# Energies of four heads in one call, with output and norm as a part of their own, in an attention and feed-forward kernel

## The chip, the cores and the metric

The kernel runs on one core of a Trainium2 chip. A core has five engines, each with its own instruction queue: TensorE (PE, matmuls, with weight loads shown apart as PEld), VectorE (DVE), ScalarE (ACT), GpSimd (POOL) and SyncE (SP, which issues DMAs). PE reads SBUF and writes PSUM, which has eight banks of 128 partitions by 2 KB; DVE and ACT empty them. The metric is the device time of one execution in microseconds (us); lower is better.

## What is computed

Eight sequences of 512 rows by 256 channels go through conditioned attention, and then through a gated mixer with a blend of decaying traces and a ternary feed-forward. Cut to what matters:

```python
y = x @ W[id].T + b[id]                       # conditioned projection
q, k, v = silu(y @ Wq), silu(y @ Wk), y @ Wv  # 16 heads of 16
q, k = [t*cos, t*sin], ...                    # 32 values a head
energy = einsum('bhnd,bhmd->bhnm', q, k) * tril
out = einsum('bhnm,bhmd->bhnd', energy, v) @ Wo * sigmoid(y @ G1 @ G2)
x = x + layernorm(out)
ctx = causal_ema(x); gated = x * sigmoid([x, ctx] @ Wg + bg)
traces = causal_ema(gated * mod[d], tau[d])   # 8 traces
gate = sigmoid(sum_d traces[d] * softmax(blend)[d] @ Wtemp + btemp)
c = layernorm((gelu(x @ Wsoma) * gate) @ Wout)
x = x + bitlinear(silu(bitlinear(c, w_gate)) * bitlinear(c, w_up), w_down)
```

There is no softmax over the energies, so attention is done in chunks of 64 rows: within a chunk by masked energies, and across chunks by a running state (the sum of k times v so far).

## The kernel before

For each sequence b there are three parts, written as Python generators that yield where they need something: `attention(b)`, `cond2(b)` (the mixer with the blend) and `ffn(b)`. A `Plan` (lines 42 to 208) simulates the engines while the program is built: `cost` and the table `MATMULS` give each instruction's duration, `add` also the time that a DMA takes. The loop at lines 1124 to 1156 always goes on with the first part, by rank, whose need is met in the plan: `ffn` has rank (1, b), `cond2` (2, b), `attention` (3, b), and the two set-ups of the weights rank (0, ...). Each engine but SP then gets the order of the plan as its fixed order (`keep`). On the chip an engine therefore works through a list and waits, with all behind it, for whatever its next instruction lacks.

Tiles come from pools of so many buffers: `p1` has one for each tag, `p2` two, `p4` four, `p6` six. PSUM is split into `ps`, four single banks (`bank`), and `ps_t`, one tile of four banks (`four_banks`). The blend takes the four-bank tile four times a sequence (`ptr`, line 972: 16 matmuls of the code, then four operations of DVE that add to `tempT`), the feed-forward four times (`pgu`, line 1066), and the set-ups in between.

Attention works on pairs of 128-row tiles, tp = 0 and 1. `project(t)` (494) makes the keys, queries and values of tile t, `turn(t, i)` (524) transposes the keys or the queries into `kT`/`qT`, `states(t, tok)` (533) adds up the running state (`sts`, `total`). `energies(tp, hh)` (570) does two of the four heads of each group: 32 matmuls into two single banks, `pes`, each multiplying 32 rows (one head's values) by 64 columns, cycling over two row groups `e` and two halves `r` of the chunk rows; then DVE multiplies each bank by the causal mask into `et`. `output(tp)` (591) multiplies energies by values, and queries by states, into two banks `po`, which ACT copies to `aT`. Then follow `pw` (aT by Wo), the gate, the norm and the residual sum into `xs`.

The body of attention (642 to 723) is one sequence: project 0, project 1, turned 0, project 2, turned 1, energies(0, 0), project 3, turned 2, energies(0, 1), output(0), the addition of beta to xs on POOL, turned 3, the gate's matmuls `pg`, energies(1, 0), `pgt`, energies(1, 1), then for tp = 0 `pw` and the norm, output(1), and the same for tp = 1. `head[b]` is set after `pg`, and lets the next sequence's attention start; `tail[b]` is set after output(1), and the next sequence's turned(1) waits for it. `cond2(b)` starts when attention(b) is done.

Of the kernel before, what the change touches and what calls it, by code (L numbers as in the profile page):

```python
# [17 lines left out]
P = 128  # L18
# [23 lines left out]
class Plan:  # L42
# [5 lines left out]

    MATMULS = {"ptr": 0.069, "po": 0.028, "pg": 0.125, "pgt": 0.26, "pm": 0.26}
    TABLES = {AF.Gelu: 1, AF.Silu: 2, AF.Exp: 3, AF.Ln: 4, AF.Sin: 5}  # L50
# [41 lines left out]
    def add(self, engine, op, args, kw, made):  # L92
# [4 lines left out]
        if op == "dma_start":  # L97
            cost = 1.2 if "transpose" in kw else 0.05
            late = math.prod(outs[0].shape) * (4 if outs[0].dtype == F32 else 2) / 230e3
        else:  # L100
            cost = self.cost(engine, op, outs[0], ins, kw)
            if engine == "tensor":
                late = 0.2
# [148 lines left out]
def adaln_attn_ffn_kernel(ctx: ExitStack, tc: tile.TileContext, a: dict, out: bass.AP):  # L252
# [22 lines left out]
    ps_t = pool("ps_t", 1, space=bass.MemoryType.PSUM)  # L275
    p1, p2, p3, p4, p6 = (pool(f"p{n}", n) for n in (1, 2, 3, 4, 6))

# [196 lines left out]
    def attention(b, xs, wt, bt):  # L474
# [19 lines left out]
        def project(t):  # L494

            tp, u = divmod(t, 2)
            pkq = bank(f"pkq_{b}_{t}")
            for k in range(KC):
                te.matmul(
                    pkq, yT[:, k, chunk(t)], wkq[:, k].rearrange("p e c -> p (e c)"), start=k == 0, stop=k == KC - 1  # L500
                )
            pv = bank(f"pv_{b}_{t}")[:, :C]
            for k in range(KC):
                te.matmul(pv, yT[:, k, chunk(t)], wv[:, k, :], start=k == 0, stop=k == KC - 1)
            sg = p2.tile([P, 2, H, HD], F32, tag="sg", name=f"sg_{b}_{t}")
# [18 lines left out]
        def turn(t, i):  # L524

            tp, u = divmod(t, 2)
            n, turned = (("k", kTs[tp]), ("q", qTs[tp]))[i]
            pt = bank(f"p{n}T_{b}_{t}")
            for g in range(NG):
                te.transpose(pt[:, chunk(g)], toks[t, i][:, chunk(g)], ident)  # L530
            ac.copy(turned[:, :, chunk(u)], pt.rearrange("p (g n) -> p g n", n=P))

        def states(t, tok):
# [35 lines left out]

        def energies(tp, hh):  # L570

            kT, qT = kTs[tp], qTs[tp]
            pes = [bank(f"pe_{b}_{tp}_{2 * hh + e}").rearrange("p (g u n) -> p g u n", g=NG, u=2) for e in range(2)]
            for g in range(NG):
                for u in range(2):
                    for e, r in ((0, 0), (1, 1), (0, 1), (1, 0)):
                        rows = slice(32 * (2 * hh + e), 32 * (2 * hh + e + 1))
                        at = slice(P * u + 64 * r, P * u + 64 * (r + 1))
                        te.matmul(
                            pes[e][64 * r : 64 * (r + 1), g, u, :], kT[rows, g, at], qT[rows, g, at], start=True, stop=True  # L580
                        )
            for e in range(2):
                et = p4.tile([P, NG, 2, 64], F32, tag="et", name=f"et_{b}_{tp}_{2 * hh + e}")
                ve.tensor_mul(
                    et.rearrange("p g u n -> p (g u) n"),
                    pes[e].rearrange("p g u n -> p (g u) n"),
                    causal.unsqueeze(1).to_broadcast([P, 2 * NG, 64]),
                )
                ets[tp, hh, e] = et

        def output(tp):
# [21 lines left out]
            for half in range(2):  # L613
                for u in range(2):
                    for e in range(2):
                        for turn in range(2):
                            for pair in range(4):
# [7 lines left out]
                                    vz[rows, u, 2 * g + hh, 2 * e : 2 * e + 2, :].rearrange("p e d -> p (e d)"),  # L625
                                    ets[tp, hh, e][rows, g, u, :],
                                    last=half == 1 and u == 1 and e == 1,
# [5 lines left out]
        def turned(t):  # L633
# [6 lines left out]
            turn(t, 1)  # L640

        project(0)
        yield needs(yT, banks=2)
# [42 lines left out]
        gates = []  # L686
# [4 lines left out]
        yield needs(kTs[1], qTs[1], banks=2)  # L691
        energies(1, 1)

        og = p1.tile([P, NT, C], F32, tag="og", name=f"og_{b}")
        for tp in range(NT // 2):
            t = 2 * tp
            if tp == 1:
                yield needs(ets[1, 1, 0], ets[1, 1, 1], sts[7], banks=2)
                output(1)
                tail[b] = True  # L700
            yield needs(aTs[tp])
            pw = bank(f"pw_{b}_{t}").rearrange("p (t c) -> p t c", t=2)
            for u in range(2):
                for k in range(KC):
                    te.matmul(
                        pw[:, u, :], aTs[tp][:, k, chunk(u)], wo[:, k, :], start=k == 0, stop=k == KC - 1
                    )
            mv = p2.tile([P, 2, 2], F32, tag="mv", name=f"mv_{b}_{t}")
            for u in range(2):

                ve.scalar_tensor_tensor(
                    og[:, t + u, :], gates[u][:, tp, :], 1.0, pw[:, u, :], ALU.add, ALU.mult
                )
                layer_stats(og[:, t + u, :], mv[:, u, :])
            rstd = layer_rstd(mv, f"rstd_a{b}_{t}")
            for u in range(2):
                ve.scalar_tensor_tensor(
                    og[:, t + u, :], og[:, t + u, :], mv[:, u, 0:1], gamma_a, ALU.subtract, ALU.mult
                )
                ve.scalar_tensor_tensor(  # L720
                    xs[:, t + u, :], og[:, t + u, :], rstd[:, u : u + 1], xs[:, t + u, :], ALU.mult, ALU.add
                )
        x2s[b] = xs

# [140 lines left out]
    def cond2(b):  # L865
# [14 lines left out]
        for k in range(KC):  # L880
            for s in range(2):
# [225 lines left out]
    wt_free = [0]  # L1107
    head, tail, begun, done = {}, {}, {}, {}
    for b in range(-1, B):
        head[b] = tail[b] = b < 0  # L1110
        for what in ("attention", "cond2", "ffn"):
            begun[b, what] = done[b, what] = b < 0
# [11 lines left out]
    while True:  # L1124
# [92 lines left out]
```

## Time and profile before

| | us |
|---|---|
| median of 3 runs | 760.28 (754.30 to 762.75) |
| profiled execution, device time | 761.35 |
| its span in the profile | 759.6 |
| PE busy | 651.3 |
| DVE busy | 509.6 |
| ACT busy | 254.4 |
| POOL busy | 216.9 |

The profile is of one execution, whose device time stands beside its span; busy times are for the whole span. Nearly all of the kernel's instructions are issued by one helper, so every row carries the same line, 221, and a group is told by its tiles: `pe<-qT,kT` are the matmuls that write the energies from qT and kT. A matmul in float32 shows as two records. Sizes are partitions by elements; for matmuls the first pair is the part of the PE array that is used (rows by columns). The output blocks, for later comparison:

```profile
L221 PE MATMUL po<-et,vz 64*32 64x64 f32 x2048 | 28.1, 238 | 13.8 <-issue 13.1
L221 DVE SCALAR_TENSOR_TENSOR tempT<-ptr,bw_c,tempT 128x512 f32<-128x512 f32 x128 | 95.8, 749 | 43.4 <-PE ptr L221 38.1
L221 PE MATMUL ptr<-dm,gated 32*128 32x128 f32 x1024 | 42.0, 304 | 21.9 <-DVE tempT L221 21.7
```

After the bar stand the busy time and the mean of one in ns, then the engine's idle time just before these instructions and what ended it.

### The profile page before, as it was taken

To read this page: it belongs to the slowest core of one execution; us is meant where nothing else is said; L and a number is where in the kernel's file an instruction comes from. 1 tells how busy PE (TensorE), PEld (TensorE's weight loads), DVE (VectorE), ACT (ScalarE), POOL (GpSimd) and SP (SyncE) were. 2 spreads that over 40 slices of the span, in tenths; PEclk is the share of its full clock that TensorE was granted. 3 is DMA by queue.
4 is the path that set the end of the run, shared out by engine and by line. 5 is a ranking of instruction groups with operands and counts; after the bars stand their busy time and mean duration, and the time that the engine had idled before them with its cause. 6 is when DMAs were issued, how large, how long until landed. Compare 5 with 4: busy or idle time off the path is not lost.

```text
span 759.6 us, 21112 instructions
## 1 busy us (share of the span) xinstructions
PE 651.3 (86%) x9330; PEld 435.4 (57%) x9330; DVE 509.6 (67%) x1015; ACT 254.4 (33%) x452; POOL 216.9 (29%) x239
## 2 busy tenths in 40 slices
PE   7689999999889988999989988999999997884453
PEld 3466666666655666566756655566766664442221
DVE  7974456876666865786666966686687667666445
ACT  3822332453224423343235322342246321410111
POOL 2740551234124231333133241333133422100000
PEclk9789999999999989999999999999999998886757
DMA  8501000121011110121011200120002100110011
GB/s 270 174 8 40 1 3 3 29 56 57 4 22 43 42 38 2 43 62 38 3 30 42 47 27 17 29 63 9 3 16 56 30 3 16 36 41 7 11 38 48
DMA packets 61196, 28.63 MB, mean 38 GB/s; under 512 B 46346, under 2 KB 60594, under 8 KB 61106
## 3 DMA queue, kind: packets, MB, share of 16 engines
q1 hardware_dynamic: 60146, 26.50, 13.1%
q8 instruction: 73, 1.20, 0.6%
q10 hardware_dynamic: 960, 0.79, 0.3%
q14 instruction: 17, 0.14, 0.1%
HBM read 12.60 MB, written 4.19 MB: 22 GB/s over the span
## 4 chain that ended last, share of the span: by engine, by line
PE 69%; DVE 18%; issue 5%; ACT 4%; DMA 3%; POOL 0%; ACTq 0%; DVEq 0%; SPq 0%; POOLq 0%
PE pgu L221 7%; PE pwg L221 6%; PE ptr L221 5%; PE po L221 5%; PE pkq L221 5%; PE py L221 4%; PE pwo L221 4%; DVE tempT L221 4%; PE ptg L221 4%; PE pd L221 4%; PE pso L221 3%; PE pe L221 3%; PE pw L221 3%; DVE h L221 2%; PE pv L221 2%
## 5 line engine op out<-in xcount | busy, mean ns | idle before, releaser
L221 DVE SCALAR_TENSOR_TENSOR tempT<-ptr,bw_c,tempT 128x512 f32<-128x512 f32 x128 | 95.8, 749 | 43.4 <-PE ptr L221 38.1
L221 POOL TENSOR_TENSOR st<-total,own 128x256 f32<-128x256 f32 x56 | 46.5, 839 | 106.2 <-DVE total L221 105.1
L221 POOL TENSOR_TENSOR ktok<-sg,cs 128x512 f32<-128x512 f32 x32 | 42.3, 1322 | 119.7 <-ACT sg L221 119.7
L221 DVE SCALAR_TENSOR_TENSOR h<-pgu,steps,sig 128x1024 f32<-128x1024 f32 x32 | 41.0, 1282 | 46.2 <-ACT sig L221 46.1
L221 PE MATMUL pkq<-wkq,yT 128*128 128x512 f32 x128 | 64.7, 628 | 0.0
L221 PE MATMUL ptr<-dm,gated 32*128 32x128 f32 x1024 | 42.0, 304 | 21.9 <-DVE tempT L221 21.7
L221 ACT ACTIVATE sig<-pgu,steps 128x1024 f32<-128x1024 f32 x32 | 35.6, 1113 | 65.3 <-PE pgu L221 60.0
L221 PE MATMUL pd<-w_downT,hqT 128*128 128x256 bf16 x256 | 37.4, 295 | 20.6 <-DMA hqT<-hq 20.6
L221 PEld LDWEIGHTS <-cqT 128*128 128x128 bf16 x256 | 26.4, 104 | 49.7 <-issue 14.9
L221 PEld LDWEIGHTS ptr<-dm,gated 32*128 32x128 f32 x1024 | 35.5, 204 | 30.0 <-issue 19.5
L221 PE MATMUL pgu<-w_gateT,cqT 128*128 128x512 bf16 x128 | 37.0, 416 | 16.1 <-DMA cqT<-cq 11.1
L221 POOL TENSOR_TENSOR qtok<-sg,cs 128x512 f32<-128x512 f32 x32 | 49.1, 1534 | 0.0
L221 POOL TENSOR_SCALAR rstd_a<-mv 128x2 f32<-128x2 f32 x16 | 6.8, 422 | 136.0 <-DVE mv L221 126.2
L221 DVE TENSOR_TENSOR et<-pe,causal 128x512 f32<-128x512 f32 x64 | 41.8, 684 | 5.5 <-PE pe L221 5.1
L221 PEld LDWEIGHTS <-hqT 128*128 128x128 bf16 x256 | 25.5, 105 | 33.8 <-DMA hqT<-hq 24.4
L221 PE MATMUL pwo<-woutT,soma 128*128 128x256 f32 x128 | 33.7, 394 | 10.7 <-ACT square L221 9.6
L221 PEld LDWEIGHTS pe<-qT,kT 32*64 32x64 f32 x2048 | 34.9, 135 | 13.7 <-issue 8.4
L221 PE MATMUL pe<-qT,kT 32*64 32x64 f32 x2048 | 40.4, 223 | 2.7 <-DVE et L221 1.1
L221 ACT ACT_TABLE_LOAD x28 | 35.9, 1283 | 19.3 <-PE pgu L221 10.5
L221 PE MATMUL po<-et,vz 64*32 64x64 f32 x2048 | 28.1, 238 | 13.8 <-issue 13.1
L221 DVE TENSOR_REDUCE hmax<-h 128x1 f32<-128x1024 f32 x32 | 38.7, 1210 | 0.3
L221 ACT COPY aT<-po 128x256 f32<-128x256 f32 x32 | 10.3, 375 | 80.3 <-PE po L221 80.3
(189 smaller groups left out, 1335.0 us busy)
## 6 DMA issues: line engine op xcount, KB each, us to landing
x<-in_x_dram SPq DMA_DIRECT2D x8, 512.0 KB, 4.5
out_dram<-res SPq DMA_DIRECT2D x32, 128.0 KB, 1.7
wt<-in_weightT_dram SPq DMA_DIRECT2D x8, 256.0 KB, 2.8
w_gateT_raw<-in_w_gateT_dram SPq DMA_DIRECT2D x2, 512.0 KB, 4.4
w_upT_raw<-in_w_upT_dram SPq DMA_DIRECT2D x2, 512.0 KB, 5.9
w_downT_raw<-in_w_downT_dram SPq DMA_DIRECT2D x2, 512.0 KB, 7.2
wgT<-in_wgT_dram SPq DMA_DIRECT2D x1, 512.0 KB, 5.1
hqT<-hq SPq DMA_TRANSPOSE x32, 2.7
```

The lines of the kernel that those rows point to most:

```text
L221: made = issue(*args, **kw)
```

## The change

Four things are changed together.

1. `energies(tp)` does all four heads of a group in one call of 64 matmuls. It writes them into the four-bank tile, one bank for each head j, and cycles over four row groups, with the two halves alternating. The mask is applied to two banks at a time.
2. Energies, output, `pw`, norm and residual become a generator of their own, `heads()`, started after turned(1) with rank (3, b, 1), behind its own attention and ahead of the next one. `ready` tells it how far the turns and the gates are. The remaining attention is projections, turns, states and gates. `outputs[b]` counts the outputs done: the next sequence's attention starts after one (and `head`), and its turned(2) after two. Energies of b wait for the whole of heads(b - 1), as do the gates; `cond2(b)` starts when heads(b) is done.
3. Buffers: `kT`/`qT` are taken when they are first turned into and not at the projection; `et` is two buffers of twice the size; `st` gets seven buffers in place of six, and `h1` one in place of two.
4. The plan's costs: 0.019 us for a matmul of the energies (the general formula gave 0.034), 0.45 us for SP to issue a DMA (0.05), and 330 GB/s for transfers (230).

```diff
-    MATMULS = {"ptr": 0.069, "po": 0.028, "pg": 0.125, "pgt": 0.26, "pm": 0.26}
+    MATMULS = {"ptr": 0.069, "pe": 0.019, "po": 0.028, "pg": 0.125, "pgt": 0.26, "pm": 0.26}
...
-            cost = 1.2 if "transpose" in kw else 0.05
-            late = math.prod(outs[0].shape) * (4 if outs[0].dtype == F32 else 2) / 230e3
+            cost = 1.2 if "transpose" in kw else 0.45
+            late = math.prod(outs[0].shape) * (4 if outs[0].dtype == F32 else 2) / 330e3
...
-                kTs[tp] = p2.tile([P, NG, 2 * P], F32, tag="kT", name=f"kT_{b}_{tp}")
-                qTs[tp] = p2.tile([P, NG, 2 * P], F32, tag="qT", name=f"qT_{b}_{tp}")
...
-            n, turned = (("k", kTs[tp]), ("q", qTs[tp]))[i]
+            n, turned = (("k", kTs), ("q", qTs))[i]
+            if u == 0:
+                turned[tp] = p2.tile([P, NG, 2 * P], F32, tag=f"{n}T", name=f"{n}T_{b}_{tp}")
...
-                    sts[c] = p6.tile([P, NG, 2, 2 * HD], F32, tag="st", name=f"st_{b}_{c}")
+                    sts[c] = p7.tile([P, NG, 2, 2 * HD], F32, tag="st", name=f"st_{b}_{c}")
...
-        def energies(tp, hh):
+        def energies(tp):
             kT, qT = kTs[tp], qTs[tp]
-            pes = [bank(f"pe_{b}_{tp}_{2 * hh + e}").rearrange("p (g u n) -> p g u n", g=NG, u=2) for e in range(2)]
+            pes = four_banks(f"pe_{b}_{tp}").rearrange("p j (g u n) -> p j g u n", g=NG, u=2)
             for g in range(NG):
                 for u in range(2):
-                    for e, r in ((0, 0), (1, 1), (0, 1), (1, 0)):
-                        rows = slice(32 * (2 * hh + e), 32 * (2 * hh + e + 1))
+                    for turn in range(2):
+                        for j in range(4):
+                            r = (j + turn) % 2
+                            rows = slice(32 * j, 32 * (j + 1))
...
-            for e in range(2):
-                et = p4.tile([P, NG, 2, 64], F32, tag="et", name=f"et_{b}_{tp}_{2 * hh + e}")
+            for hh in range(2):
+                et = p2.tile([P, 2, NG, 2, 64], F32, tag="et", name=f"et_{b}_{tp}_{hh}")
...
+        def heads():
+            for tp in range(NT // 2):
+                yield needs(
+                    kTs.get(tp, xs),
+                    qTs.get(tp, xs),
+                    four=True,
+                    when=lambda: ready["energies"] > tp and written(kTs[tp], qTs[tp]) and done[b - 1, "heads"],
+                )
+                energies(tp)
+                yield needs(ets[tp, 0], ets[tp, 1], sts[4 * tp + 3], banks=2)
+                output(tp)
+                outputs[b] = tp + 1
+                if tp == 0:
+                    gp.tensor_add(xs, xs, beta_a.unsqueeze(1).to_broadcast([P, NT, C]))
+                    og = p1.tile([P, NT, C], F32, tag="og", name=f"og_{b}")
+                yield needs(aTs[tp], when=lambda: ready["gates"])
...
+            x2s[b] = xs
...
         project(2)
-        yield needs(when=lambda: tail[b - 1])
         yield from turned(1)
-        yield needs(kTs[0], qTs[0], banks=2)
-        energies(0, 0)
+        ready["energies"] = 1
+        start((3, b, 1), b, "heads", heads(), lambda: True)
         yield needs(yT, banks=2)
         project(3)
+        yield needs(when=lambda: outputs[b - 1] == 2)
         yield from turned(2)
-        yield needs(kTs[0], qTs[0], banks=2)
-        energies(0, 1)
-        yield needs(ets[0, 1, 0], ets[0, 1, 1], sts[3], banks=2, when=lambda: done[b - 1, "attention"])
-        output(0)
-
-        gp.tensor_add(xs, xs, beta_a.unsqueeze(1).to_broadcast([P, NT, C]))
         yield from turned(3)
+        ready["energies"] = 2
...
         head[b] = True
-        yield needs(kTs[1], qTs[1], banks=2)
-        energies(1, 0)
-        yield needs(g1T, banks=2)
+        yield needs(g1T, banks=2, when=lambda: done[b - 1, "heads"])
...
+        ready["gates"] = True
...
-        h1 = p2.tile([P, T // 2], F32, tag="h1", name=f"h1_{b}")
+        h1 = p1.tile([P, T // 2], F32, tag="h1", name=f"h1_{b}")
...
-        if b < B and b in loaded and head[b - 1]:
+        if b < B and b in loaded and head[b - 1] and outputs[b - 1]:
...
-        if b < B and done[b, "attention"] and done[b - 1, "cond2"] and done[0, "setup_cond2"] and done[0, "setup_ffn"]:
+        if b < B and done[b, "heads"] and done[b - 1, "cond2"] and done[0, "setup_cond2"] and done[0, "setup_ffn"]:
```

More of the change, by code (lines that the diff above doesn't have):

```diff
@@ L275, in adaln_attn_ffn_kernel @@
     ps_t = pool("ps_t", 1, space=bass.MemoryType.PSUM)
-    p1, p2, p3, p4, p6 = (pool(f"p{n}", n) for n in (1, 2, 3, 4, 6))
+    p1, p2, p3, p4, p7 = (pool(f"p{n}", n) for n in (1, 2, 3, 4, 7))
     def bank(name, dtype=F32):
@@ L530, in turn @@
                 te.transpose(pt[:, chunk(g)], toks[t, i][:, chunk(g)], ident)
-            ac.copy(turned[:, :, chunk(u)], pt.rearrange("p (g n) -> p g n", n=P))
+            ac.copy(turned[tp][:, :, chunk(u)], pt.rearrange("p (g n) -> p g n", n=P))
         def states(t, tok):
@@ L568, in attention @@
         ets, aTs = {}, {}
-        def energies(tp, hh):
+        def energies(tp):
             kT, qT = kTs[tp], qTs[tp]
-            pes = [bank(f"pe_{b}_{tp}_{2 * hh + e}").rearrange("p (g u n) -> p g u n", g=NG, u=2) for e in range(2)]
+            pes = four_banks(f"pe_{b}_{tp}").rearrange("p j (g u n) -> p j g u n", g=NG, u=2)
             for g in range(NG):
                 for u in range(2):
-                    for e, r in ((0, 0), (1, 1), (0, 1), (1, 0)):
-                        rows = slice(32 * (2 * hh + e), 32 * (2 * hh + e + 1))
[L578 to L581, printed above, removed]
-            for e in range(2):
-                et = p4.tile([P, NG, 2, 64], F32, tag="et", name=f"et_{b}_{tp}_{2 * hh + e}")
+                    for turn in range(2):
+                        for j in range(4):
+                            r = (j + turn) % 2
+                            rows = slice(32 * j, 32 * (j + 1))
+                            at = slice(P * u + 64 * r, P * u + 64 * (r + 1))
+                            te.matmul(
+                                pes[64 * r : 64 * (r + 1), j, g, u, :], kT[rows, g, at], qT[rows, g, at], start=True, stop=True
+                            )
+            for hh in range(2):
+                et = p2.tile([P, 2, NG, 2, 64], F32, tag="et", name=f"et_{b}_{tp}_{hh}")
                 ve.tensor_mul(
-                    et.rearrange("p g u n -> p (g u) n"),
-                    pes[e].rearrange("p g u n -> p (g u) n"),
-                    causal.unsqueeze(1).to_broadcast([P, 2 * NG, 64]),
+                    et.rearrange("p e g u n -> p (e g u) n"),
+                    pes[:, 2 * hh : 2 * hh + 2].rearrange("p e g u n -> p (e g u) n"),
+                    causal.unsqueeze(1).to_broadcast([P, 4 * NG, 64]),
                 )
-                ets[tp, hh, e] = et
+                ets[tp, hh] = et
         def output(tp):
@@ L625, in output @@
                                     vz[rows, u, 2 * g + hh, 2 * e : 2 * e + 2, :].rearrange("p e d -> p (e d)"),
-                                    ets[tp, hh, e][rows, g, u, :],
+                                    ets[tp, hh][rows, e, g, u, :],
                                     last=half == 1 and u == 1 and e == 1,
@@ L640, in turned @@
             turn(t, 1)
+        gates = []
+        ready = {"energies": 0, "gates": False}
+        def heads():
[5 more added lines that the diff above has]
+                    when=lambda: ready["energies"] > tp and written(kTs[tp], qTs[tp]) and done[b - 1, "heads"],
+                )
+                energies(tp)
[6 more added lines that the diff above has]
+                yield needs(aTs[tp], when=lambda: ready["gates"])
+                t = 2 * tp
+                pw = bank(f"pw_{b}_{t}").rearrange("p (t c) -> p t c", t=2)
+                for u in range(2):
+                    for k in range(KC):
+                        te.matmul(
+                            pw[:, u, :], aTs[tp][:, k, chunk(u)], wo[:, k, :], start=k == 0, stop=k == KC - 1
+                        )
+                mv = p2.tile([P, 2, 2], F32, tag="mv", name=f"mv_{b}_{t}")
+                for u in range(2):
+                    ve.scalar_tensor_tensor(
+                        og[:, t + u, :], gates[u][:, tp, :], 1.0, pw[:, u, :], ALU.add, ALU.mult
+                    )
+                    layer_stats(og[:, t + u, :], mv[:, u, :])
+                rstd = layer_rstd(mv, f"rstd_a{b}_{t}")
+                for u in range(2):
+                    ve.scalar_tensor_tensor(
+                        og[:, t + u, :], og[:, t + u, :], mv[:, u, 0:1], gamma_a, ALU.subtract, ALU.mult
+                    )
+                    ve.scalar_tensor_tensor(
+                        xs[:, t + u, :], og[:, t + u, :], rstd[:, u : u + 1], xs[:, t + u, :], ALU.mult, ALU.add
+                    )
+            x2s[b] = xs
         project(0)
@@ L685, in attention @@
                 te.matmul(pgts[u][:, tp, :], g1T[rows, chunk(tp)], g2[rows, :], start=True, stop=True)
-        gates = []
         for r in range(2):
@@ L690, in attention @@
             gates.append(gate)
[L691 to L723, printed above, removed]
+        ready["gates"] = True
     def setup_cond2():
@@ L1107, in adaln_attn_ffn_kernel @@
     wt_free = [0]
-    head, tail, begun, done = {}, {}, {}, {}
+    head, outputs, begun, done = {}, {}, {}, {}
     for b in range(-1, B):
-        head[b] = tail[b] = b < 0
-        for what in ("attention", "cond2", "ffn"):
+        head[b], outputs[b] = b < 0, 2 * (b < 0)
+        for what in ("attention", "heads", "cond2", "ffn"):
             begun[b, what] = done[b, what] = b < 0
```

## The prediction

> **What bounds the kernel now.** I read the page from the top: span, the 40 slices, the chain, then the groups. After that I asked for busy time by stage, for the waits of PE alone, and for the order of time around a few blocks.
>
> ```profile
> span 759.6 us, 21112 instructions
> PE   7689999999889988999989988999999997884453
> DVE  7974456876666865786666966686687667666445
> PEclk9789999999999989999999999999999998886757
> PE 69%; DVE 18%; issue 5%; ACT 4%; DMA 3%; POOL 0%; ACTq 0%; DVEq 0%; SPq 0%; POOLq 0%
> ```
>
> Each digit is one slice of 19 us. PE is full from slice 4 to slice 33, DVE at six to seven tenths. After that PE falls to half: the last batch's blend and feed-forward run there alone, and no attention is left to fill their gaps. The last line, the chain of waits by engine, has PE at 69%. Split at 85 and 640 us (columns: length, then busy us and count of PE, weight load, DVE, ACT, POOL; then granted clock, DMA share, GB/s):
>
> ```profile
> 0.00:85.00 85.00, 68.37 (x979) 44.80 (x980) 62.27 (x134) 36.61 (x65) 39.14 (x48) 0.90 0.36 110
> 85.00:640.00 555.00, 513.92 (x7996) 353.13 (x7994) 381.99 (x760) 197.55 (x358) 172.28 (x182) 0.98 0.11 28
> 640.00:760.00 120.00, 68.99 (x356) 37.50 (x356) 65.32 (x123) 20.21 (x30) 5.44 (x9) 0.72 0.13 31
> ```
>
> In the middle stage PE works 513.9 of 555 us, so a microsecond of PE work taken out there is nearly a microsecond of the kernel. Its 41.1 us of idle time are small, by PE's own waits in that stage (total, times, longest):
>
> ```profile
> PE ptr L221 <- DVE tempT L221: 11.6, 9, 2.1
> PE po L221 <- issue: 11.0, 8, 2.1
> PE pwo L221 <- ACT square L221: 8.3, 14, 0.6
> ...
> PE pe L221 <- DVE et L221: 1.1, 4, 0.3
> ```
>
> The last 120 us hold no attention, so the change can only move them as a whole.
>
> **The energies' matmuls.** The groups that the change touches, and their nearest neighbours (busy us, mean ns of one, then idle before):
>
> ```profile
> L221 PE MATMUL pe<-qT,kT 32*64 32x64 f32 x2048 | 40.4, 223 | 2.7 <-DVE et L221 1.1 <-DVE total L221 1.0 <-ACT qT L221 0.6
> L221 DVE TENSOR_TENSOR et<-pe,causal 128x512 f32<-128x512 f32 x64 | 41.8, 684 | 5.5 <-PE pe L221 5.1
> L221 DVE SCALAR_TENSOR_TENSOR h<-pgu,steps,sig 128x1024 f32<-128x1024 f32 x32 | 41.0, 1282 | 46.2 <-ACT sig L221 46.1
> ```
>
> A float32 matmul of the code is two records, so 32 calls of 64 records take 40.4 us, 1.26 us each. One block and, for comparison, an output block in the order of time:
>
> ```profile
> 200.39 1.16 PE L221 MATMUL pe<-qT,kT 32*64 32x64 f32 x64
> ...
> 215.39 1.43 PE L221 MATMUL po<-et,vz 64*32 64x64 f32 x122
> 218.93 0.31 PE L221 MATMUL po<-et,vz 64*32 64x64 f32 x6 [2.10 <-issue]
> ```
>
> An energies record takes 1.16/64 = 18 ns, an output record 1.43/122 = 11.7 ns, although both stream 64 columns. The start times inside the blocks say why. In energies four records start 7 ns apart, then 39 ns pass: 59 ns for four, because the code cycles over two row groups by two column halves, four places of the array. Output cycles over eight places, and at its best eight start 7 ns apart with the next eight 57 to 58 ns after the first. The change makes energies cycle over four row groups by two halves, also eight places. So 128 records of a call should come as 16 groups at some 59 ns, what 64 records take now: 16 calls at 1.26 us = 20.2 us instead of 40.4. Bounds: saving 0 if the pace per record stays at 18 ns, 40.4 - 2048 x 13.7 ns = 12.3 us if output's mean over the run holds (28.1 us for 2048 records, slow stretches in it), 20.2 if the best pace holds. I take 20.2: the interleaving is that of output's best stretch, and the operands are stored as in today's block. Where does it land? The energies have 33.65 us of their PE time in the middle stage and 6.75 in the first, by the same windows for them alone. Half of 33.65 is 16.8, taken whole; of the 3.4 in the first stage, where PE is busy 68.4 of 85 us, I count half, 1.7. **Sum: -18.5 us.**
>
> The Trainium skill, page "TensorE: Matmul & The Clock Gate", section "Wait — 56ns, not 53.3ns?", speaks against this: starts of matmuls never come closer than about 25 ns, however small they are. Today's 18 ns and 11.7 ns per record are already below that, so the rows decide; read per matmul of the code, 1024 x 25 ns = 25.6 us would save 5 us less than I say and give 747.
>
> **Fetching instructions.** The 2.10 us before the last six output records are put down to "issue": nothing that the profile shows was awaited. This comes in long runs of short instructions: the instruction queue moves 16 KB blocks, and over the run 73 of them make the 1.20 MB beside 18,660 PE records, some 256 records each. A new energies call is 128 matmuls and 128 weight loads, about one block in 1.2 us. Today's half calls show no such wait of the matmuls before pe. Bounds: 0, or the mean output stall, 11.0/8 = 1.4 us, at all 16 calls, 22 us. I take 0.13 us a call, **+2**, near today's row of none, since the number of instructions is unchanged and slow projections lie between.
>
> **The mask on DVE.** 64 operations at 684 ns become 32 over two banks. Nearest row of that shape is h, 1282 ns: 41.0 instead of 41.8 us. DVE is 69% busy in the middle, so it is counted at nothing; its cover is DVE's 173 us of idle time there.
>
> **The four banks as a meeting place.** Energies leave two of the four single banks and take the one group of four that the blend (ptr) and the feed-forward (pgu) also use. A call holds it for 1.26 us of matmuls and two masks of 1.28 us, with gaps 4 us. The order of PE is fixed ahead, so where the plan believes the group free and DVE is late, PE stands with all behind it: projections, turns, pwo. Today's instance:
>
> ```profile
> 275.90 0.68 DVE L221 TENSOR_TENSOR et<-pe,causal 128x512 f32<-128x512 f32 x1
> 276.13 2.09 PE L221 MATMUL ptr<-dm,gated 32*128 32x128 f32 x32 [2.12 <-DVE tempT L221]
> ```
>
> Here a mask on DVE delayed the blend's own reads, and PE stood 2.12 us. In the middle 28 ptr blocks lose 11.6 us, 0.41 each. The 14 new users there at that rate: **+5.8**; bounds 0 and 14 x 2.12 = 30.
>
> The skill's "TensorEngine Tiling (Array Packing)", section "PSUM Bottleneck", warns that tiling speeds up the matmuls and not the emptying of their banks. The rows agree in kind (1.26 us to fill, 2.6 to empty four banks); were emptying to set the pace everywhere, the saving would vanish and the time stay near 760.
>
> **Energies, output and norm as a part beside.** Projections and turns no longer stand in line with energies and output. The new part may start output(0) while project(3) and later turns wait, and the next batch gets as far as its turned(2) before the old batch's second output, where turned(1) was the limit. In the blend stage PE so has more to put before a late ptr. I take two thirds of the 11.6 us, **-8**; bounds -12 (all of it) and 0. The moves inside it issue what they did: the addition of beta on POOL (8 x 2.42 us, POOL is 29% busy), gates, pw, norm; no DMA changes place on SP's queue. Buffers: kT and qT taken at the turn, one more st, one h1 less. h1's next writer comes about 70 us later, so nothing waits; st gains slack. The new costs of transfers alter the planned order alone. They matter at the start, where PE waits 2.0, 0.7 and 2.5 us for weight sums: bounds -5 and +5, taken 0.
>
> **Sum:** -18.5 + 2 + 5.8 - 8 = -18.7 us. The profiled execution took 761.35 us, 1.75 more than its span, and the median shown is 760.28: 740.9 in the span, 742 on the median.
>
> **Rivals.**
>
> (A) As summed: 742, its own range 733 to 752 (waits and refilling vary). Chance 0.58.
>
> (B) More: all of the ptr waits refilled, no new waits, 2 us at the start: -18.5 - 12 - 2 = -32, 728. For it speaks that only 41 us of the middle are idle and the new part is free to fill them. Against: 8.3 us are waits of pwo for ACT and 11.0 for instructions, which nothing here touches. 0.12.
>
> (C) The eight places bring nothing, since loading weights or fetching limits the pace, as in output's slow stretches: 0 + 2 + 5.8 - 8, so 760. For it: output's mean is 13.7 ns, not 7.4. Against: its best stretches. The change then does not do what it says. 0.14.
>
> (D) Slower: the group of four banks becomes the bound. In the middle, 14 calls hold it 4 us each, 56 us. The blend's four uses follow each other at 4.4 us through a stage of some 17 us (100.7 to 118.3 in the first batch), so it is taken there nearly without a gap, and feed-forward's uses follow soon. If PE stands for half of that: +28 + 2 - 18.5 = +11.5, 772. It decides once PE's waits for DVE before ptr, pgu and pe exceed today's 13 us by about 20. Against: the blend has the higher rank and will take the group first, and PE has projections meanwhile. 0.16.
>
> About 1% (752.7 to 767.9) is what a measurement can tell from no change. Faster: A but its edge 0.56, B 0.12, a little of C 0.04: 0.72. Same: A's edge 0.02, most of C 0.10, D's lower part 0.03: 0.15. Slower: 0.13. The range of 726 to 764 leaves out some 0.04 of B and most of D.
>
> **What would show it.** Right: pe near 20 us in 16 blocks of 128 records at 1.2 to 1.3 us; et 32 times near 1.28 us; PE busy near 631; the middle 15 to 20 us shorter, the last 120 us unchanged. Fetching: "issue" before pe. The meeting place: waits of pe for DVE, and of ptr and pgu for et. It would be wrong if pe stays near 40 us (C), or if PE's idle time in the middle grows beyond 60 us (D).

## The result and the profile after

| | us |
|---|---|
| median after, 20 runs | 764.10 (759.91 to 772.90) |
| median before on the same chip, 20 runs | 759.59 (754.30 to 763.98) |
| after by before, 95% interval | 1.0059 (1.0038 to 1.0080) |
| profiled execution after, device time | 760.01 |
| its span | 758.3 |
| PE busy, and idle within the span | 636.4, 121.9 (before 651.3, 108.3) |

The forecast of 742 was wrong, and 764.1 lies just outside its range: the kernel is 4.5 us slower on the median, 0.6%, small but clear of noise. Medians are of all runs, and ratios leave out the few that ran in a slower state (one of after, one of E6, three of E8, one of the before beside E9 to E12). The two profiled executions differ the other way (760.0 after, among the fastest of its 20, and 761.4 before), so they show what became of the saving and not the last 4.5 us. In them 14.9 us of PE work are gone and PE's idle time is 13.6 us longer. Most of this study asks where that idle time comes from.

The page of the kernel after, span, slices and chain:

```profile
span 758.3 us, 21057 instructions
...
PE   7688999999998989999978999998888856965453
...
DVE  7875445698557967577757957668579854677445
...
PE 67%; DVE 18%; issue 5%; ACT 4%; DMA 3%; POOL 1%; SPq 0%; ACTq 0%; POOLq 0%; DVEq 0%
```

Its groups (busy us, mean ns of one, idle before):

```profile
L221 PE MATMUL pe<-qT,kT 32*64 32x64 f32 x2048 | 25.8, 231 | 1.4 <-issue 1.4
...
L221 DVE TENSOR_TENSOR et<-pe,causal 128x1024 f32<-128x1024 f32 x32 | 38.0, 1216 | 6.6 <-PE pe L221 6.1
```

The energies fell by 14.6 us, the mask by 3.8. By stage (columns as before: length, busy us and count of PE, weight load, DVE, ACT, POOL; clock, DMA share, GB/s):

```profile
0.00:85.00 85.00, 64.27 (x970) 42.15 (x971) 60.79 (x128) 31.92 (x60) 36.89 (x48) 0.88 0.35 110
85.00:640.00 555.00, 502.48 (x7992) 341.50 (x7990) 387.26 (x722) 199.85 (x355) 166.00 (x181) 0.97 0.12 28
640.00:760.00 120.00, 69.63 (x371) 37.93 (x370) 68.54 (x133) 22.43 (x39) 6.14 (x11) 0.76 0.13 31
```

The middle stage holds nearly as many PE records as before, 7992 to 7996, so the same work still needed the same 555 us, with 11.4 us less of it busy. PE's own waits there (total, times, longest):

```profile
PE ptr L221 <- DVE tempT L221: 15.5, 8, 4.8
PE po L221 <- issue: 10.8, 8, 1.6
PE pwo L221 <- ACT square L221: 7.1, 12, 0.6
PE ptg L221 <- DVE tempT L221: 6.0, 3, 2.2
PE pgu L221 <- DVE h L221: 3.9, 3, 1.7
...
PE pe L221 <- issue: 1.4, 1, 1.4
```

No pe waits for a DVE mask, as rival D would have it. What grew are waits inside the blend, `ptr` by 3.9 us and `ptg` to 6.0, and those of the feed-forward's `pgu`, 3.9 (no such row before). Most of the time of `ptr` is lost late: the stretch from 580 to 640 us, before and after:

```profile
580.00:640.00 60.00, 54.37 (x1067) 40.72 (x1065) 41.19 (x86) 17.95 (x37) 18.86 (x21) 0.97 0.07 18
```

```profile
580.00:640.00 60.00, 42.30 (x588) 28.02 (x586) 40.48 (x74) 14.14 (x20) 5.50 (x7) 0.86 0.11 27
```

PE does 12 us less in these 60 us, with half the records and a third of POOL's work: attention has run out. The timelines say why. Each blend opens with `px2T<-ident,x`, the transposes of what attention left in x. DVE writes the last x here, in before and in after:

```profile
643.31 0.88 DVE L221 SCALAR_TENSOR_TENSOR x<-og,rstd_a,x 128x256 f32<-128x256 f32 x2 [0.90 <-POOL rstd_a L221]
```

```profile
622.02 0.48 DVE L221 SCALAR_TENSOR_TENSOR x<-og,rstd_a,x 128x256 f32<-128x256 f32 x1 [0.60 <-POOL rstd_a L221]
623.09 0.47 DVE L221 SCALAR_TENSOR_TENSOR x<-og,rstd_a,x 128x256 f32<-128x256 f32 x1
```

And the last blend on PE begins here, before and after (in the second, the blend ahead of it is shown as well):

```profile
645.05 1.91 PE L221 MATMUL px2T<-ident,x 128*128 128x128 f32 x8
```

```profile
619.91 1.21 PE L221 MATMUL ptr<-dm,gated 32*128 32x128 f32 x32 [2.26 <-DVE tempT L221]
...
625.94 2.09 PE L221 MATMUL ptr<-dm,gated 32*128 32x128 f32 x32 [4.82 <-DVE tempT L221]
631.35 2.09 PE L221 MATMUL ptr<-dm,gated 32*128 32x128 f32 x32 [3.32 <-DVE tempT L221]
...
646.00 1.04 PE L221 MATMUL px2T<-ident,x 128*128 128x128 f32 x8
```

The last attention ends at 623.6 instead of 644.2 us, 20.6 earlier, a little more than the forecast took off the whole kernel. But the last blend does not begin earlier, and its start sets the time: in all 16 traces of this study the span ends 111 to 117 us after it. `cond2(7)` may start only when `cond2(6)` is done, and that one ran late: it began at 578.4, before at 568.1. Its `ptr` stand 2 to 5 us each for DVE, with no attention left to fill them.

Blend 6 is late because its x was (575.4; before 564.5). PE's timeline shows sequence 6 between its first and its second call of energies:

```profile
477.44 1.59 PE L221 MATMUL pe<-qT,kT 32*64 32x64 f32 x128
...
505.41 1.48 PE L221 MATMUL po<-et,vz 64*32 64x64 f32 x128
...
512.64 1.03 PE L221 MATMUL pgu<-w_gateT,cqT 128*128 128x512 bf16 x4
...
523.18 1.17 PE L221 MATMUL ptr<-dm,gated 32*128 32x128 f32 x32
...
531.24 1.29 PE L221 MATMUL ptr<-dm,gated 32*128 32x128 f32 x32 [2.29 <-DVE tempT L221]
...
543.31 1.17 PE L221 MATMUL ptr<-dm,gated 32*128 32x128 f32 x32
...
550.49 1.59 PE L221 MATMUL pe<-qT,kT 32*64 32x64 f32 x128
```

Before, sequence 6 had its four calls within 27 us (517.7 to 545.2). Now 73 us lie between two. The first 33 or so are the new part's own order: `output` and `pw` come between the calls, `pw` at 508.3. In the other 40 its keys and queries are ready (the last copy to `qT` ends at 487.4), and the four-bank tile goes through a series of feed-forward and blend uses. Sequences 1, 2 and 4 have 32, 41 and 73 us there, sequences 3, 5 and 7 34 to 36.

The blends start at 82, 162, 252, 320, 416, 484, 578 and 646 us in after. These intervals of 68 to 96 us are no more uneven than those of before (71 to 99), but what the blends wait for has changed. Before, each begins within 4 us of its last x, and the last `pwo` of the blend ahead (the matmuls that close a blend on PE) has ended 12 to 35 us earlier. In after, blends 2, 4 and 6 begin 3 us after their last x, and 3, 5 and 7 only 21 to 22 us after it, directly behind the `pwo` of the blend ahead.

### The profile page after: what moved, and what is told of

Its sections match the earlier page's. It is cut to its first block, busy times and chain, and to the rows that moved or that the text cites. A ratio compares the mean times of both kernels' runs of the same rounds, so it can differ in the third digit from the quotient of the medians.

```text
span 758.3 us, 21057 instructions
## 1 busy us (share of the span) xinstructions
PE 636.4 (84%) x9330; PEld 421.6 (56%) x9330; DVE 516.6 (68%) x983; ACT 254.2 (34%) x452; POOL 209.0 (28%) x239
## 3 DMA queue, kind: packets, MB, share of 16 engines
q1 hardware_dynamic: 60146, 26.50, 13.7%
## 4 chain that ended last, share of the span: by engine, by line
PE 67%; DVE 18%; issue 5%; ACT 4%; DMA 3%; POOL 1%; SPq 0%; ACTq 0%; POOLq 0%; DVEq 0%
PE pgu L221 8%; PE pwg L221 6%; PE pkq L221 5%; DVE tempT L221 5%; PE ptr L221 4%; PE pwo L221 4%; PE pw L221 4%; PE po L221 4%; PE pso L221 4%; PE ptg L221 4%; PE pd L221 3%; PE py L221 3%; PE pv L221 2%; DVE h L221 2%; PE pe L221 2%
## 5 line engine op out<-in xcount | busy, mean ns | idle before, releaser
L221 PE MATMUL pkq<-wkq,yT 128*128 128x512 f32 x128 | 66.7, 646 | 0.4 <-ACT kT L221 0.4
L221 DVE SCALAR_TENSOR_TENSOR h<-pgu,steps,sig 128x1024 f32<-128x1024 f32 x32 | 41.0, 1282 | 32.9 <-ACT sig L221 32.9
L221 PE MATMUL ptr<-dm,gated 32*128 32x128 f32 x1024 | 41.4, 302 | 22.0 <-DVE tempT L221 19.4
L221 POOL TENSOR_TENSOR st<-total,own 128x256 f32<-128x256 f32 x56 | 43.1, 774 | 58.4 <-DVE total L221 58.3
L221 PE MATMUL pd<-w_downT,hqT 128*128 128x256 bf16 x256 | 39.8, 307 | 22.2 <-DMA hqT<-hq 20.6
L221 PEld LDWEIGHTS ptr<-dm,gated 32*128 32x128 f32 x1024 | 35.0, 203 | 33.9 <-issue 26.2
L221 PEld LDWEIGHTS <-cqT 128*128 128x128 bf16 x256 | 25.8, 103 | 48.0 <-issue 18.6
L221 POOL TENSOR_TENSOR qtok<-sg,cs 128x512 f32<-128x512 f32 x32 | 43.2, 1350 | 0.0
L221 DVE TENSOR_TENSOR et<-pe,causal 128x1024 f32<-128x1024 f32 x32 | 38.0, 1216 | 6.6 <-PE pe L221 6.1
L221 PE MATMUL ptg<-tempT,wtempT 128*128 128x512 f32 x64 | 32.9, 649 | 7.7 <-DVE tempT L221 7.7
L221 DVE TENSOR_REDUCE hmax<-h 128x1 f32<-128x1024 f32 x32 | 38.8, 1214 | 0.4
L221 POOL TENSOR_SCALAR rstd<-squares 128x2 f32<-128x2 f32 x16 | 3.1, 192 | 129.0 <-ACT square L221 129.0
L221 ACT ACTIVATE sg<-pkq 128x512 f32<-128x512 f32 x32 | 19.1, 598 | 57.6 <-PE pkq L221 57.6
L221 PE MATMUL po<-et,vz 64*32 64x64 f32 x2048 | 26.3, 225 | 13.0 <-issue 13.0
L221 ACT COPY qT<-pqT 128x512 f32<-128x512 f32 x32 | 18.7, 586 | 52.7 <-PE pqT L221 52.7
```

The source lines that it names most:

```text
L221: made = issue(*args, **kw)
```

## The experiments

All times are medians against before on the same chip (759.6 to 761.1), ratios with their 95% intervals.

**Which part costs?** Energies of before (two heads a call, two single banks) inside the changed structure; the four-head energies inside the old sequence; the new transfer costs alone in the kernel before; and, in the changed kernel, energies first at the four-bank tile.

E2, from after:

```diff
-    MATMULS = {"ptr": 0.069, "pe": 0.019, "po": 0.028, ...}
+    MATMULS = {"ptr": 0.069, "po": 0.028, ...}
-                    four=True,
+                    banks=2,
-                energies(tp)
-                yield needs(ets[tp, 0], ets[tp, 1], sts[4 * tp + 3], banks=2)
+                energies(tp, 0)
+                yield needs(banks=2)
+                energies(tp, 1)
+                yield needs(ets[tp, 1, 0], ets[tp, 1, 1], sts[4 * tp + 3], banks=2)
```

> The changed kernel with the energies of before: two heads a call in two single banks, two calls for a tile pair, all else as changed. PE's energies return from 25.8 to about 40 us. Theory 1: the group no longer holds the energies up, so in spite of 14 us more of PE work it is no slower than the changed kernel, 745 to 760. Theory 2: the loss stays and the PE work is added: 768 to 780. Theory 3 (the plan's transfers made a worse order): also 768 to 780.

E3, from before (energies as in the change):

```diff
-        yield needs(kTs[0], qTs[0], banks=2)
-        energies(0, 0)
...
-        energies(0, 1)
+        yield needs(kTs[0], qTs[0], four=True)
+        energies(0)
...
-        energies(1, 0)
...
-        energies(1, 1)
+        yield needs(kTs[1], qTs[1], four=True)
+        energies(1)
```

> The kernel before with only the four-head energies in the four-bank group; the body of attention stays one sequence, and transfers are planned as before. Theory 1: the whole attention, projections too, stands behind the group, so it is slower than before, 765 to 790. Theory 2: PE's saving of about 15 us arrives, 742 to 752. Theory 3: as theory 2.

E4, from before:

```diff
-            cost = 1.2 if "transpose" in kw else 0.05
-            late = ... / 230e3
+            cost = 1.2 if "transpose" in kw else 0.45
+            late = ... / 330e3
```

> The kernel before with only the plan's two costs of transfers changed (0.45 us for an issue, 330 GB/s). Theory 3: this alone is slower than before by 8 us or more, 768 to 780. Theories 1 and 2: the order at the start changes a little and the time is within 6 us of before, 754 to 766.

E1, from after:

```diff
+                wants[b] = lambda tp=tp: ready["energies"] > tp and written(kTs[tp], qTs[tp]) and done[b - 1, "heads"]
...
+                del wants[b]
                 energies(tp)
...
-                yield needs(dm, gated, four=True)
+                yield needs(dm, gated, four=True, when=lambda: not wanted())
...
-            yield needs(cqT[:, t], four=True)
+            yield needs(cqT[:, t], four=True, when=lambda: not wanted())
```

> The changed kernel, but blend and feed-forward leave the four-bank group alone whenever a sequence's energies are ready for it. Theory 1 (the energies stand behind the group: in the changed kernel the second energies call of sequence 6 came 73 us after the first, and its x2 at 575 us where the old one had it at 565): the second calls come within 40 us of the first, x2 of sequences 2, 4 and 6 comes 10 us or more earlier, PE's idle time at 580 to 640 us falls from 17.7 us to under 10, and the time falls to 740 to 752. Theory 2 (the part's own order and rank are the loss, not the group): the calls come earlier but the time stays at 757 to 770.

| | us | ratio |
|---|---|---|
| E2 | 779.53 | 1.0287 (1.0207 to 1.0367) |
| E3 | 802.24 | 1.0554 (1.0474 to 1.0634) |
| E4 | 754.08 | 0.9918 (0.9882 to 0.9955) |
| E1 | 773.80 | 1.0174 (1.0092 to 1.0255) |

Four heads at once are worth having within the new part (E2 is 15.4 us slower than after) and ruinous in the old sequence (E3), where by the order of the body all that follows in an attention stands behind a call that needs all four banks: the second calls of sequences 4 and 6 come 72 and 68 us after the first. The transfer costs alone, which I had at nothing, bring 6 us. E1 shows that the tile was what held the energies, and that freeing it does not help: these second calls now come 22 and 36 us after the first, and the last x of sequences 1, 2 and 6 at 147.5, 226.5 and 558.6 us instead of 162.0, 249.0 and 575.4. But the blends stand 82.6 us apart on average (80.6 in after), and the last starts at 660. Who gets the banks first moves the loss, and here made it 9.7 us larger.

**Is it the order, or the transfer costs?** The same two-head instructions at three ranks of the new part, and the four-head kernel at rank 2, then with the old transfer costs.

```diff
-        start((3, b, 1), b, "heads", heads(), lambda: True)
+        start((2, b, 1), b, "heads", heads(), lambda: True)
```

E5 is this in E2; E6 is this in after; E8 is E2 with rank (0, b, 1); E7 is after with the transfer costs of before (0.05 and 230e3).

> The two-head kernel of e2 with one edit: heads() gets rank (2, b, 1), behind its blend rank but ahead of its own attention's projections. Theory 2, sharpened (the part's low rank leaves its chain of short steps for last, so x2 and with it the blend come late and in pairs): the blends start at even distances of about 80 us and the 25 us that the part cost come back, 745 to 758. If another piece of the part is the cause (buffers, the gates' wait, the start of the next attention), it stays at 770 to 785.

> The changed kernel with the same one edit, rank (2, b, 1) for heads(). Theory 2: x2 comes earlier and evenly, PE's saving arrives, 738 to 752. Theory 1 (the four-bank group is the bound, whoever takes it first): the energies still find the group taken by the blend and feed-forward or hold these up; the blends stay in pairs or grow longer, 757 to 775.

> The changed kernel with the plan's old costs of transfers (0.05 us, 230 GB/s). If the 6 us that e4 won by the new costs belong to the start, this is slower than the changed kernel by about 6 us, 767 to 775. If they only fell out of another order, the sign is open, 750 to 780.

> The two-head kernel of e2 with heads() ahead of everything but the set-ups, rank (0, b, 1). Theory 2: as e5 or better, 738 to 755, since two-head energies in single banks hold up nobody's four-bank group. If taking PE from the blend and the feed-forward costs more than early x2 brings: 760 to 775.

| | us | ratio |
|---|---|---|
| E5 | 789.18 | 1.0381 (1.0293 to 1.0469) |
| E6 | 754.03 | 0.9892 (0.9799 to 0.9986) |
| E7 | 751.74 | 0.9897 (0.9863 to 0.9932) |
| E8 | 760.64 | 0.9990 (0.9940 to 1.0041) |

E2, E5 and E8 hold the same instructions and lie 28.5 us apart, more than the whole saving on PE: the order alone does that. The same edit makes two heads 10 us slower (E5) and four heads 10 us faster (E6). And the transfer costs, which gave 6 us in the old sequence, take 12.4 from the changed kernel (E7).

**Where do the transfer costs bite, is unevenness the loss, and what does the part alone do?** E10 uses the old costs in the plan's first 40 us only. E9 puts E1's rule on the blend alone and adds the edits of E6 and E7, so that the blends come evenly. E11 is E2 with the old transfer costs: the part alone. E12 is E6 with them.

```diff
+            early = self.now < 40.0
-            cost = 1.2 if "transpose" in kw else 0.45
-            late = ... / 330e3
+            cost = 1.2 if "transpose" in kw else (0.05 if early else 0.45)
+            late = ... / (230e3 if early else 330e3)
```

> The changed kernel with the old costs of transfers for those issued in the first 40 us of the plan, the new costs after. If the 12 us between the changed kernel (764.1) and e7 (751.7) come from the start, where the new costs bring the weights too early into the plan: 750 to 757. If they come from the steady part: 760 to 768.

> The changed kernel with the old costs of transfers (as e7, 751.7), rank (2, b, 1) for heads() (as e6), and the blend, but not the feed-forward, leaving the four-bank group to energies that are ready. Theory 4 (PE's saving is real, and is lost because blends come in pairs, so that at the end the last blend waits for the one before it while the last attention is long done): in the planned order the blends are spaced evenly; if so on the chip, PE's idle time at 580 to 640 us falls from 19 to under 10 us and the time is 735 to 748. Theory 5 (any order of these parts costs what it wins, since the chip does not follow the plan): 750 to 770.

> The part beside alone: two-head energies in single banks and the old costs of transfers, thus e2 (779.5) without the new costs, or the kernel before with the part. If the part itself costs what e2 shows over e4 (25 us) and the costs of transfers add to it: 768 to 785. If e2's loss came of the new costs and the part together: 752 to 765.

> The changed kernel with both edits that helped singly, the old costs of transfers (e7, 751.7) and rank (2, b, 1) for heads() (e6, 754.0). If their gains of 12 and 10 us add up: 740 to 746. If both only undo the same loss (pairs of blends or a late start): 748 to 756.

| | us | ratio |
|---|---|---|
| E10 | 756.02 | 0.9935 (0.9893 to 0.9977) |
| E9 | 754.19 | 0.9907 (0.9865 to 0.9949) |
| E11 | 771.17 | 1.0125 (1.0081 to 1.0169) |
| E12 | 749.49 | 0.9820 (0.9786 to 0.9855) |

The plan's first 40 us account for 8 of the 12.4 us (E10), and not through PE's order: block for block it is that of after, and DVE, ACT and POOL are ordered otherwise only in the first 37 us. The first blend begins at 75.7 us in place of 81.8. E9 has its blends 73 to 88 us apart, starting from 79.9 to 640.6, and still takes 754: evenness is not what was missing, and that explanation falls. From blend 2 on each x is ready 6 to 22 us ahead and each blend begins directly behind the last, so there the blends don't wait for attention. The part alone, with its buffers, costs 11 us (E11; 10 against before on its own chip). E12 has the lowest median, 11.6 us under before on its chip. It shares the shape of the loss, though. The same late stretch of E12:

```profile
580.00:640.00 60.00, 41.49 (x578) 26.32 (x578) 44.07 (x86) 12.32 (x23) 4.28 (x8) 0.89 0.14 28
```

Its last x is done at 616.4 us and its last blend begins at 635.1. Every kernel with four heads a call is so (E6 622.9 and 641.1, E7 618.3 and 640.8, E9 619.1 and 640.6; over all nine the blend is 18 to 31 us behind). In the seven with two heads a call the two lie within 3 us: E4 has 639.9 and 639.1, there the blend begins before the last x is complete. In all nine the last blend begins directly behind the `pwo` of the one ahead, so with four heads the chain of blends sets its start. In before, E4, E5 and E13 that `pwo` has ended 10 to 12 us earlier, and attention sets the start; in E2, E8 and E11 the two come together.

**Does PE still bound the kernel?** If not, adding PE work to the changed kernel would cost less than adding it to before. All energies are issued twice (the second pass writes the same values again), in before (E13) and in after (E14), with the plan's cost halved so that the order stays.

```diff
-            for g in range(NG):
+            for g in [*range(NG), *range(NG)]:
```

> The kernel before with every matmul of the energies issued twice into the same place, and each planned at half its cost, so that the order of all engines stays as it is: 40 us of PE work are added and nothing else. If PE bounds the kernel before, as the prediction said: 793 to 803. If a chain through several engines bounds it and PE has room: under 780.

> The changed kernel in the same way, its energies' matmuls issued twice at the same order: 26 us of PE work are added, somewhat more than the change saved. If PE still bounds the changed kernel (its saving was spent elsewhere, in the start and in the order): 785 to 792. If the saving is lost because PE's work is no longer what bounds it and the chain from blend to blend does: 764 to 776.

E13 took 796.17 us (1.0448, 1.0385 to 1.0512), E14 826.93 (1.0849, 1.0794 to 1.0904): +36 on before and +62.8 on after. The groups of the two, E13 first:

```profile
L221 PE MATMUL pe<-qT,kT 32*64 32x64 f32 x4096 | 72.3, 222 | 3.4 <-issue 2.5 <-ACT qT L221 0.7
```

```profile
L221 PE MATMUL pe<-qT,kT 32*64 32x64 f32 x4096 | 52.0, 233 | 27.8 <-issue 27.8
```

E13 added 31.9 us of matmuls and the kernel grew by 36. E14 added 26.2 us of matmuls and 26.4 us of waiting for instructions, 52.6 in all, and grew by 62.8. In E14 the rest of PE's work was slower too, 631.6 us in place of 610.5, at a mean granted clock of 0.902 (0.930 in after); in E13 it was not (610.4 and 610.9 before, at 0.932 and 0.931). So PE has no time to spare in either kernel: a block added to its list delays the end in full. That doesn't tell PE as a whole from the chain of blends, since such a block also stands ahead of the blends' own instructions in PE's fixed order. In E14 too that chain ended last, with the last x done at 693.5 us and the last blend begun at 717.9. One block of E14 on PE's timeline shows the term of waiting:

```profile
245.05 2.40 PE L221 MATMUL pe<-qT,kT 32*64 32x64 f32 x205
...
249.03 0.80 PE L221 MATMUL pe<-qT,kT 32*64 32x64 f32 x51 [1.58 <-issue]
```

After 205 records PE stood 1.58 us for nothing that PE's view of the profile shows; each of the 16 blocks did so once. By the DMA records each of these waits ended 1.3 to 1.6 us after a 16 KB packet of the instruction queue had come in, as did the one in after. E14 overshot both of its expectations, neither of which had this term; E1, E3 and E5 too came out above all that was expected of them.

## Why the prediction was wrong

The sum is -18.5 + 2 + 5.8 - 8; the runs add up, in medians, as before 760 → 771.2 (the part, E11) → 751.7 (four heads in it, E7) → 764.1 (transfer costs): +11, -19.4, +12.4. These sizes depend on the sequence in which the edits are made: the transfer costs are -6, +8.4 (E11 to E2) or +12.4.

- **The energies' matmuls, -18.5.** Right in kind, too large: 14.6 us (40.4 to 25.8). Blocks take 1.59 us, not 1.26. The best eight starts are 7 ns apart with the next eight 58 to 59 ns on, as forecast, but that pace comes only twice in a block; the other eights take 66 to 167 ns, 8 to 21 ns a record. The best stretch was no price for a block; the mean of output, 13.7 ns, which I set as the other bound, was nearer to the 12.6 found. The rule cited from the page "TensorE: Matmul & The Clock Gate", section "Wait — 56ns, not 53.3ns?", gives 25.6 us as an estimate, and 25.8 was measured; the starts 7 ns apart contradict its floor all the same, so the agreement of the sums is no confirmation.
- **Fetching, +2.** Right: one wait of 1.4 us. E14 shows that the room was small: twice the block, and every block waits.
- **The mask.** 1216 ns against 1282 taken: a few us of DVE time, off the path as said.
- **The four banks, +5.8.** The hold of 4 us was right (4.28 on average), the form of the loss wrong. I looked for PE standing at pe, ptr and pgu; the plan sees the tile taken and orders the energies behind whole series of blend and feed-forward instead. The price is then not a wait in PE's list but a sequence whose second half comes 73 us after its first, which no row of PE's waits shows. Rival D had the place, and priced it as waits; its sign did not come (PE idles 52.5 us in the middle, not over 60).
- **The part beside, -8.** This is the step that failed: alone it costs 11 us (E11), so it was off by 19 and had the wrong sign. I refilled today's `ptr` waits with work that the new structure *may* put there, without working out what it does to the order of the rest. E2, E5 and E8 show that rank alone moves such a kernel by 28 us. In E11 attention and blends both came later: the last x at 658.7 us (644.2 before), 2 us more for each sequence, and the last blend at 656.0 (645.1), directly behind the one ahead. Which of the part's edits, or of its buffers, makes this stays open; in E11, `po` waits 7.6 us for masks and `px2T` 7.6 for x.
- **The transfer costs, 0 within 5.** In the sequence -6, at the edge of the bounds; here +12.4, far outside them. They were bounded by three waits of PE at the start. The start was the right place for 8 of the 12.4 us (E10), but the loss came by the order of DVE, ACT and POOL there, which the bounds left out. The other 4 (E10 to E7) go with a different order between 194 and 281 us alone.
- **The last 120 us unchanged.** In the window from 640 us that is so (69.6 us of PE work, 69.0 before). But attention ended 20.6 us earlier and the last blend 1 us later, so the stretch in which blend and feed-forward run without cover grew by these 22 us. That is where most of the saving went, as idle time of PE: 17.7 us between 580 and 640 us (5.6 before), and 20.7 in the first 85 us (16.6), with 2.6 less in the rest of the span.

"A microsecond of PE work taken out in the middle is nearly a microsecond of the kernel" held when work was added (E13, E14), not here: what was taken out was attention, and once attention was done sooner, the chain of blends set the end, which did not become shorter. From the first blend to the last there are 80.9 us each in before, 80.6 in after, with 1.9 us less PE work for each sequence (14.9/8), and 80.1 in E9. Why E9's even blends keep that pace stays open; so does how far a plan could be brought to turn all of the saving into time.

## What to carry to other kernels

Work removed from a busy engine counts only if the chain that sets the end moves up too: before the sum, follow the last few start times of that chain back, and ask whether the removed work was on it or was its filling. Where instructions get their order from a plan, edits of ranks, costs or shared buffers can move the time by as much as the planned saving, in either direction (here by 6 to 28 us, against 18.7); try the neighbouring ranks and costs with it, since here the same change at rank 2 with the old transfer costs ran 11.6 us under the kernel before (E12) instead of 4.5 over. A pace read from the best stretch of a block is a bound, and the mean over blocks the price.

## What the hardware showed beside this

The sums of DVE that close attention became slower, though their instruction didn't change: 806 ns on average, 599 before. One tile's instructions in after, from 230 to 250 us (shortest, median and longest in ns):

```profile
L221 DVE SCALAR_TENSOR_TENSOR x<-og,rstd_a,x x2: 471/1534/2597, 246.0 to 248.5; 128x256 f32<-128x256 f32 x2
```

The first ran beside POOL's addition to x, which began at 246.0 us too and took 2.38 us, and needed 2597 ns; the second, alone, 471. Of the 32, 11 overlap work of POOL (median 1492 ns), the other 21 don't (476). Not each of the 11 is slowed: three took over 2580 ns, all beside that addition, four 1492 to 1495, and four 466 to 549; the two shortest had begun before the POOL instruction that overlaps them most. The Trainium skill, page "GPSIMD Engine Reference", section "8. Key points", has POOL sharing its SBUF interfaces with VectorE, with contention where a DVE instruction has two SBUF inputs; this one has two, and seven of the 11 rows agree. Masks and `tempT`, which read PSUM, were not slowed so: their medians are 1214 and 750 ns beside POOL as without it.

And 512 short PE instructions in a row, 256 matmul records and as many weight loads (E14), waited for instructions in all 16 blocks, by 1.74 us on average (27.8/16), where half as many (after) did so in one block of 16.
